# A four-layer attention and expert kernel: expert stages issued in a written order, two blocks a step, with up weights loaded three steps ahead

## The chip, the cores and the metric

The kernel runs on one core of one Trainium2 chip. The metric is the device time of one execution in microseconds (us), the median of several runs. Times inside the kernel come from one profiled execution. PE is the matmul engine (TensorE), DVE is VectorE, ACT is ScalarE, POOL is GpSimd, and SP is the engine whose queue issues the plain DMAs here.

## The reference, cut to what matters

`x` has 4 batches of 512 tokens of width 128; the context `ctx_1024` has 4 batches of 154 rows. Four layers each add an attention and an expert network to `x`, always on a normalised `x`:

```python
x = x + _L0_xattn_ref(_layernorm(x), ctx, ...)      # similarity of width 154, four feature groups @ W_qv
x = x + _L0_ffn_ref(_layernorm(x), ...)             # top 2 of 8; (x@W0+b0) * silu(x@W1+b1) @ W2 + b2, 512 hidden
x = x + _L1_xattn_ref(ctx, ctx, _layernorm(x), mask, ...)   # 16 heads of 8
x = x + _L1_ffn_ref(_layernorm(x), ...)             # top 1 with a capacity; gelu(x@W1+b1) @ W2 + b2, 512 hidden
x = x + _L2_xattn_ref(_layernorm(x), ctx, ...)      # 16 heads of 64, gated by tanh
x = x + _L2_ffn_ref(_layernorm(x), ...)             # top 2; gelu(x@w1) @ w2, 256 hidden, no biases
x = x + _L3_xattn_ref(_layernorm(x), ctx, ctx, ...) # 16 heads of 64
x = x + _L3_ffn_ref(_layernorm(x), ...)             # top 2; relu(x@W1+b1) @ W2 + b2, 512 hidden
```

All arithmetic on data is float32.

## The kernel before, in words

`x` lies in SBUF for the whole run, one tile per batch, four token tiles of 128 in each. A layer has these stages.

**Attention.** In layers 1 to 3 `attend_all` runs 16 periods, one for a token tile. A period (`narrow_period`, L431, for layer 1; `wide_period`, L486, for 2 and 3) writes out by hand the order of PE, ACT and DVE: scores and exponentials of the new tile beside transposes, the product with the values and the projection of the old one. `tc.manual_schedule` (L1280) keeps that order on PE, ACT and DVE. SP and POOL are placed by the framework. Each period also takes up to two steps of the work beside it (`middle`, `after`): the rest of the layer before, or the routing of the first half.

**Routing** (`route`, L647) for a half, which is two batches or 1024 tokens: statistics (L224 to L233, a power on POOL), normalisation (L240), transposes, logits (L662), the best one or two experts (`top`, L622), ranks, and from them a slot for each token in a buffer in DRAM that is sorted by expert and cut in blocks of 128. One expert owns a block. A list `eb` (L741) gives the expert of each block. The half has 23 blocks, in layer 1 it has 15. Sixteen indirect DMAs of 128 rows (8 in layer 1) scatter the tokens into the buffer (L718, on POOL). They are put in a list, `rows_due`, and `row_transfers` starts them two at a time, each behind some copy.

**Experts** (`experts`, L821). A block goes through `up` (L850): the expert's number is read into registers of SP and PE, its up weights are loaded with its biases behind them in the same rows (L861; 516 KB in layer 0, 258 KB in layers 1 and 3, 128 KB in layer 2; three buffers), and PE multiplies (L872) into `sc`, a PSUM tile of two banks, double buffered. Then `down` (L877): activation into `hT` (in layer 0 ACT computes silu from bank 1 of `sc`, L887, and DVE multiplies it with bank 0, L888; in layer 3 two pieces are done on DVE, L894, and two on ACT, L896), the product with the down weights (L899), a copy on DVE (`ys`, L907) and a store (L908). Every float32 product of 128x128 is two matmul instructions in the trace.

**Combining.** Sixteen indirect DMAs (8 in layer 1) gather the results (L932, on POOL) and DVE adds them to `x` with the weights of the experts (L950).

The halves overlap: the experts of half 0 run beside the routing of half 1, the experts of half 1 beside the gathers of half 0, the statistics and the preparation of the next attention. The gathers of half 1 run beside the next attention. Outside `attend_all` the framework's scheduler orders all engines, by readiness in a timeline of its own, so it may put an instruction of one stage between those of another.

**Constants.** Small parameters arrive in some 20 small DMAs; the context is transposed on PE (L193 to L202), some parameters too (L209, L1067, L1076).

The framework follows data in SBUF by regions and adds the waits between engines.

Of the kernel before, what the change touches and what calls it, by code (L numbers as in the profile page):

```python
# [9 lines left out]
F32 = mybir.dt.float32  # L10
# [36 lines left out]
def tile_xattn_moe_stack(ctx: ExitStack, tc: tile.TileContext, a: dict, out: bass.AP):  # L47
# [94 lines left out]
    wide_ends = const.tile([P, 4, P], F32, name="wide_ends")  # L142
    nc.gpsimd.memset(wide_ends, 0.0)
# [31 lines left out]
    nth = const.tile([1, BLK[0], E], F32, name="nth")  # L175
# [4 lines left out]
    def row_bc(src, n, name):  # L180

        t = const.tile([P, n], F32, name=name)
        nc.sync.dma_start(t, src.partition_broadcast(P))
        return t


    ctxT = const.tile([P, B, S2], F32, name="ctxT")
    ct4 = const.tile([P, B, 4, ST], F32, name="ct4")
    ct2 = const.tile([P, B, 64], F32, name="ct2")
    nc.gpsimd.memset(ct2, 0.0)  # L190
    tp = ps_tr()
    for b in range(B):
        nc.tensor.transpose(tp[:, b * P : (b + 1) * P], cm[:, b, :], ident)  # L193
    nc.vector.tensor_copy(ctxT[:, :, 0:P], tp.rearrange("p (b k) -> p b k", b=B))
    tp = ps_tr()
    for b in range(B):
        nc.tensor.transpose(tp[:, b * ST : (b + 1) * ST], ctail[:, b, :], ident[:ST, :ST])
    tpv = tp[:, 0 : B * ST].rearrange("p (b k) -> p b k", b=B)
    nc.vector.tensor_copy(ctxT[:, :, P:S2], tpv)
# [3 lines left out]

    def columns(src, rows, name):

        t = p2.tile([rows, P], F32, tag="rows", name=f"{name}_r")
        nc.sync.dma_start(t, src)
        q = ps_tr()
        nc.tensor.transpose(q[:, 0:rows], t, ident[:rows, :rows])  # L209
        o = const.tile([P, rows], F32, name=name)  # L210
        nc.vector.tensor_copy(o, q[:, 0:rows])
        return o
# [54 lines left out]
    class Tile:  # L267
# [8 lines left out]
        def __init__(self, at, i):  # L276
            self.at, self.i = at, i
            self.per = P // at.dh
            self.nb = H // self.per
            self.pr = p2.tile([P, H, S2], F32, tag="probs", name="probs")  # L280
            self.nm = small.tile([P, H], F32, tag="nm", name="nm")
            self.rs = small.tile([P, H], F32, tag="rs", name="rs")
            self.sc, self.q, self.pT, self.av = {}, {}, {}, {}
# [28 lines left out]
        def short(self):  # L312
            if self.nb == 1:
                self.ends = p2.tile([P, 4, T4], F32, tag="short", name="short", bufs=1)
                nc.scalar.copy(self.ends.rearrange("p g (h k) -> p (g h) k", h=4), self.pr[:, :, P:S2])
            else:
                self.ends = wide_ends
                for r in range(2):
                    nc.scalar.copy(
                        wide_ends[:, :, 64 * r : 64 * r + 2 * ST].rearrange("p c (s k) -> p c s k", s=2),  # L320
                        self.pr[:, 8 * r : 8 * r + 8, P:S2].rearrange("p (c s) k -> p c s k", s=2),
                    )
# [5 lines left out]
        def replicate(self):  # L328
# [5 lines left out]
            self.rep = p2.tile([P, self.nb, P], F32, tag="rep", name="rep")  # L334
# [21 lines left out]
        def take_ends(self, engine):  # L356
            self.tails = p2.tile([self.rows, 4, P], F32, tag="tails", name="tails")
            copy(engine, self.tails.rearrange("p g q -> p (g q)"), self.q["ends"][0 : self.rows, :])
# [72 lines left out]
    def narrow_period(new, old, middle=nothing, queries=nothing, parts=nothing, after=nothing):  # L431
# [37 lines left out]
        middle()  # L469
        if old:  # L470
            old.by_v(2)
            old.by_v(3)
            old.scaled(0)
        if new:
# [11 lines left out]
    def wide_period(new, old, middle=nothing, queries=nothing, parts=nothing, after=nothing):  # L486
# [24 lines left out]
        if old:  # L511
            old.scaled(0)
            old.by_v(3)
        middle()
        if old:
            old.scaled(1)
# [17 lines left out]
    def attention64(b, gather_x, wq, wk, wv, wo, add):  # L534
# [51 lines left out]
        def queries(i):  # L586
            at.qT[i] = t = p3.tile([P, 8, P], F32, tag="t8", name="qT")
# [49 lines left out]
    def row_transfers(n=2 * NH, behind=None):  # L637

        for start in rows_due[:n]:
# [6 lines left out]

    def route(layer, half, wg, bg, b2):  # L647
# [4 lines left out]
        lg = rsm("lg", NH, E)  # L652
# [18 lines left out]
        ohs, ws = [oh1], []  # L671
# [5 lines left out]
        else:  # L677
# [4 lines left out]
            ohs.append(oh2)  # L682
            nc.vector.tensor_tensor(sel[:, 0:NH, :], oh1, oh2, ALU.add)
# [18 lines left out]
        nc.vector.tensor_reduce(first, t4, AX.X, ALU.add)  # L702
        yield
        base = rsm("base", NH, E)
        nc.vector.scalar_tensor_tensor(base, bc(first, 1, NH), float(P), rk[:, 0:NH, :], ALU.mult, ALU.add)
        slots = []
# [8 lines left out]
        scatters = []  # L715
# [18 lines left out]
        end = rt.tile([1, E], F32, tag="end", name="end")  # L734
        nc.vector.tensor_tensor(end, first[0:1], nb[0:1], ALU.add)
        t6 = rt.tile([1, BLK[0], E], F32, tag="t6", name="t6", bufs=1)
        nc.vector.tensor_tensor(t6[:, 0:nj, :], bc(end, 1, nj), nth[:, 0:nj, :], ALU.is_le)
        ef = rt.tile([1, BLK[0]], F32, tag="ef", name="ef")
        nc.vector.tensor_reduce(ef[:, 0:nj], t6[:, 0:nj, :], AX.X, ALU.add)
        eb = rt.tile([1, BLK[0]], I32, tag="eb", name="eb")  # L740
        nc.vector.tensor_scalar(eb[:, 0:nj], ef[:, 0:nj], float(E - 1), None, ALU.min)  # L741

        if layer == 1:
# [9 lines left out]
            if half:  # L753
                nc.vector.tensor_tensor(rg, rk[:, 0:NH, :], bc(seen[0], 1, NH), ALU.add)
                nc.vector.tensor_tensor(rg, rg, oh1, ALU.mult)
            else:
                seen.append(tot)
                nc.vector.tensor_tensor(rg, rk[:, 0:NH, :], oh1, ALU.mult)
# [4 lines left out]
            ws.append(wa)  # L763
        else:
            d = rsm("d", NH)
            nc.vector.tensor_tensor(d, m2, m1, ALU.subtract)
# [8 lines left out]
            ws += [wa, wb]  # L775
        yield
        if b2 is not None:

            comb = rsm("comb", NH, E)
            nc.vector.tensor_tensor(comb, ohs[0], bc(ws[0], 2, E), ALU.mult)  # L780
            if len(ws) > 1:
                t7 = rsm("t7", NH, E)
                nc.vector.tensor_tensor(t7, ohs[1], bc(ws[1], 2, E), ALU.mult)
# [10 lines left out]
            for k, cT in enumerate(cTs):  # L794
                y = ps_av()
                for i in range(NI):
                    nc.tensor.matmul(
                        y[:, i * D : (i + 1) * D], cT[:, i * P : (i + 1) * P], b2, start=True, stop=True
                    )
                xb = x[2 * half + k]  # L800
                nc.vector.tensor_tensor(xb, xb, y.rearrange("p (i d) -> p i d", i=NI), ALU.add)
        return eb, list(zip(ws, slots)), scatters
# [11 lines left out]
    def load_down(layer):  # L814

        t = w1.tile([P, E, 4, D], F32, tag="w2", name="w2")
        nf = NF[layer]
        nc.sync.dma_start(t[:, :, 0:nf, :], a[f"down{layer}"].rearrange("p (e c d) -> p e c d", e=E, c=nf))
        return t

    def experts(layer, half, routed, w2):  # L821

        ebs, _, scatters = routed
        nj, nf, nu = BLK[layer == 1], NF[layer], UPS[layer]
        pack = a[f"up{layer}"]
        width = pack.shape[2]
        bias = nu * nf * P
        loaded, toks = {}, {}
# [12 lines left out]
        def tokens(g):  # L841
# [4 lines left out]
            tokT = wff.tile([P, 4 * P], F32, tag="tokT", name="tokT", bufs=2)  # L846
            evac(tokT[:, 0 : m * P], q[:, 0 : m * P])
            toks[g] = tokT

        def up(j):  # L850

            xT = toks[j // 4][:, (j % 4) * P : (j % 4 + 1) * P]
            e = nc.values_load(
                ebs[0:1, j : j + 1],
                engines=[mybir.EngineType.SP, mybir.EngineType.PE],
                min_val=0,
                max_val=E - 1,
                skip_runtime_bounds_check_because="a count of at most E - 1, by a minimum",
            )
            w = wff.tile([P, 1032], F32, tag="w", name="w")  # L860
            nc.sync.dma_start(w[:, 0:width], pack[bass.ds(e, 1), :, :].rearrange("o p n -> p (o n)"))  # L861
            sc = ps_sc()
            for u in reversed(range(nu)):
                for fc in range(nf):
                    at = (u * nf + fc) * P
                    if layer == 0:
                        dst = sc[:, u, fc * P : (fc + 1) * P]
                    elif layer == 3:
                        dst = sc[:, fc // 2, fc % 2 * P : (fc % 2 + 1) * P]
                    else:  # L870
                        dst = sc[:, 0, fc * P : (fc + 1) * P]
                    nc.tensor.matmul(dst, w[:, at : at + P], xT, start=True, stop=True)  # L872
            return e, w, sc
# [3 lines left out]
        def down(j, e, w, sc):  # L877
            hT = p3.tile([P, nf, P], F32, tag="hT", name="hT")
            if layer == 2:
                nc.scalar.activation(hT.rearrange("p f t -> p (f t)"), sc[:, 0, 0 : nf * P], AF.Gelu)  # L880
            for fc in range(nf if layer != 2 else 0):
                up = sc[:, 0, fc * P : (fc + 1) * P]
                b0 = w[:, bias + fc : bias + fc + 1]
                if layer == 0:
                    g = p2.tile([P, P], F32, tag="eg", name="eg", bufs=4)
                    b1 = w[:, bias + nf + fc : bias + nf + fc + 1]
                    nc.scalar.activation(g, sc[:, 1, fc * P : (fc + 1) * P], AF.Silu, bias=b1)  # L887
                    nc.vector.scalar_tensor_tensor(hT[:, fc, :], up, b0, g, ALU.add, ALU.mult)  # L888
                elif layer == 1:
                    nc.scalar.activation(hT[:, fc, :], up, AF.Gelu, bias=b0)  # L890
                else:
                    up = sc[:, fc // 2, fc % 2 * P : (fc % 2 + 1) * P]
                    if fc < 2:
                        nc.vector.tensor_scalar(hT[:, fc, :], up, b0, 0.0, ALU.add, ALU.max)  # L894
                    else:
# [491 lines left out]
```

## Time and profile before

| | |
|---|---|
| median of 3 runs | 1358.62 us (1355.46 to 1359.36) |
| the profiled execution | 1354.62 us |
| its span, first to last instruction | 1352.8 us |
| mean clock granted to PE | 0.93 |
| busy: PE, its weight loads, DVE, ACT, POOL | 1113.4, 908.6, 770.9, 568.8, 252.9 us |
| DMA | 126.81 MB, mean 94 GB/s |

The stages lie at these times in the trace, read from the first and last of their instructions:

| layer | attention | experts: first token transpose, half 0 | half 1 | first exponential of the next attention |
|---|---|---|---|---|
| 0 | 0 | 116.5 | about 204 | 291.7 |
| 1 | 291.7 | 512.1 | 562.0 | 605.0 |
| 2 | 605.0 | 846.1 | 908.4 | 955.3 |
| 3 | 955.3 | 1203.4 | 1267.6 | end 1352.8 |

In the profile "busy" is the time of instructions on an engine, "idle before" the time the engine stood still just before a group of instructions, and the name after the arrow is what that idle time ended with. Ends of matmuls are modelled, so a busy PE is not a PE at its peak.

### The profile page before, as it was taken

Reading aid. Unit: us, or ns where it says so; the run is one execution under the profiler, and the core shown is the slowest. Engines: PE = TensorE matmul, PEld = TensorE weight load, DVE = VectorE, ACT = ScalarE, POOL = GpSimd, SP = SyncE. Lnnn points to the kernel's source line nnn. Section 1 sums busy time; section 2 is a strip of 40 time slices with the busy share of each in tenths; the row PEclk is TensorE's granted clock in tenths of the full one; section 3 lists DMA queues with packets and bytes.
Section 4 is the critical chain, followed back from the end, with each engine's and each line's share of the span. In section 5 each row is a group of like instructions: output and inputs, shape, how many; then the busy total and the mean of one; then the engine's idle time right before and its main releaser. Section 6 shows DMA issues by size and latency. Waiting matters only on the chain.

```text
span 1352.8 us, 26947 instructions
## 1 busy us (share of the span) xinstructions
PE 1113.4 (82%) x9435; PEld 908.6 (67%) x9435; DVE 770.9 (57%) x2089; ACT 568.8 (42%) x2258; POOL 252.9 (19%) x281
## 2 busy tenths in 40 slices
PE   4885988887777788889999988868899998889891
PEld 3775887764334347777778777756777777679881
DVE  5563645557766764245666776425477576646452
ACT  1112443455454444455555455212555555433230
POOL 2022213104000020312000003045120000402424
PEclk8786998999898988998999999879999999989996
DMA  7013675551101214532112213444421111335762
GB/s 216 0 63 107 184 232 153 167 170 40 21 19 28 63 40 112 147 108 79 33 33 55 57 36 105 114 147 129 126 60 43 33 33 33 86 82 146 203 186 61
DMA packets 136995, 126.81 MB, mean 94 GB/s; under 512 B 13466, under 2 KB 116511, under 8 KB 136479
## 3 DMA queue, kind: packets, MB, share of 16 engines
q1 hardware_dynamic: 129695, 110.39, 29.4%
q0 software_dynamic: 7168, 14.69, 3.6%
q8 instruction: 78, 1.28, 0.4%
q14 instruction: 54, 0.44, 0.1%
HBM read 101.31 MB, written 23.72 MB: 92 GB/s over the span
## 4 chain that ended last, share of the span: by engine, by line
PE 35%; DVE 8%; DMA 6%; ACT 4%; issue 4%; POOL 3%; SPq 0%; POOLq 0%; DVEq 0%; ACTq 0%
PE sc L605 5%; PE tr L421 5%; PE av L404 4%; PE tr L367 4%; PE sc L872 4%; DMA w<-in_up 3%; PE av L899 3%; PE sc L590 3%; ACT probs L304 2%; DVE nm L292 2%; PE av L386 2%; DVE pT L261 2%; POOL yg L932 1%; PE sc L554 1%; POOL buf L718 1%
## 5 line engine op out<-in xcount | busy, mean ns | idle before, releaser
L304 ACT ACTIVATE probs<-sc,nm 128x154 f32<-128x154 f32 x768 | 286.1, 404 | 266.1 <-DVE nm L292 265.8
L872 PE MATMUL sc<-tokT,w 128*128 128x128 f32 x1528 | 213.9, 289 | 29.2 <-DMA w<-in_up 22.8
L872 PEld LDWEIGHTS sc<-tokT,w 128*128 128x128 f32 x1528 | 192.9, 200 | 43.3 <-issue 11.4
L899 PE MATMUL av<-w,hT 128*128 x1160 | 175.0, 284 | 11.4 <-DVE hT L888 8.5
L292 DVE TENSOR_REDUCE nm<-sc 128x6 f32<-128x924 f32 x144 | 142.9, 1009 | 68.1 <-PE sc L605 34.0
L304 ACT ACTIVATION_READ_ACCUMULATOR probs<-sc,nm 128x1 f32 x768 | 170.2, 222 | 0.0
L899 PEld LDWEIGHTS av<-w,hT 128*128 128x128 f32 x1160 | 150.4, 194 | 23.0 <-DVE hT L888 12.7
L932 POOL DMA_INDIRECT yg<-ybuf,su x112 | 107.6, 960 | 277.6 <-DVE pT L261 132.6
L261 DVE COPY pT<-tr 128x512 f32<-128x512 f32 x192 | 128.0, 687 | 52.3 <-PE tr L367 49.3
L233 POOL TENSOR_TENSOR rstd<-ve,nhalf 128x4 f32<-128x4 f32 x32 | 32.9, 1030 | 652.7 <-DVE ve L231 598.6
L718 POOL DMA_INDIRECT buf<-xn,su x112 | 108.1, 965 | 163.5 <-DVE eb L741 42.1
L367 PE MATMUL tr<-ident,probs 128*128 128x128 f32 x768 | 117.2, 287 | 13.3 <-DVE pT L261 13.3
L367 PEld LDWEIGHTS tr<-ident,probs 128*128 128x128 f32 x768 | 84.9, 144 | 40.3 <-DVE pT L261 20.4
L404 PE MATMUL av<-pT,vm 128*64 128x128 f32 (+1 forms) x1536 | 104.8, 286 | 7.1 <-DVE pT L261 7.1
L887 ACT ACTIVATE eg<-sc,w 128x128 f32<-128x128 f32 x184 | 66.2, 367 | 94.5 <-DVE hT L888 72.7
L907 DVE COPY ys<-av 128x128 f32<-128x128 f32 x168 | 48.5, 289 | 82.8 <-PE av L899 75.5
L888 DVE SCALAR_TENSOR_TENSOR hT<-sc,w,eg 128x128 f32<-128x128 f32 x184 | 63.0, 348 | 51.2 <-ACT eg L887 48.6
L404 PEld LDWEIGHTS av<-pT,vm 128*64 128x64 f32 (+1 forms) x1536 | 65.0, 128 | 35.9 <-issue 20.5
L605 PE MATMUL sc<-kT,qT 64*128 64x154 f32 x1024 | 85.1, 304 | 3.5 <-ACT probs L304 3.5
L605 PEld LDWEIGHTS sc<-kT,qT 64*128 64x128 f32 x1024 | 69.8, 186 | 13.3 <-ACT probs L304 7.7
L421 PE MATMUL tr<-wo,aT 128*128 128x128 f32 x512 | 67.1, 284 | 9.3 <-ACT tails L264 6.8
L590 PE MATMUL sc<-xnT,wq 128*128 128x128 f32 x512 | 71.0, 296 | 2.9 <-ACT probs L304 2.9
(251 smaller groups left out, 1460.6 us busy)
## 6 DMA issues: line engine op xcount, KB each, us to landing
w<-in_up SPq DMA_DIRECT2D x46, 516.0 KB
w<-in_up SPq DMA_DIRECT2D x76, 258.0 KB
rep<-rd SPq DMA_DIRECT2D x64, 256.0 KB
ybuf<-ys SPq DMA_DIRECT2D x168, 64.0 KB
tok<-buf SPq DMA_DIRECT2D x36, 256.0 KB
w<-in_down SPq DMA_DIRECT2D x3, 2048.0 KB
w<-in_up SPq DMA_DIRECT2D x46, 128.0 KB
buf<-zero SPq DMA_DIRECT2D x2, 1472.0 KB
```

The costliest lines, as they stand in the source:

```text
L261: return nc.vector.tensor_copy(o, i)
L292: nc.vector.tensor_reduce(self.at.heads(self.nm, g, n), self.sc[g][:, :, 0 : n * S2].rearrange("p j (s k) -> p j s k", s=n), AX.X, ALU.max ...
L304: nc.scalar.activation(self.pr[:, h, :], self.sc[g][:, j, s * S2 : (s + 1) * S2], AF.Exp, bias=self.nm[:, h : h + 1], accum_out=self.rs[:, ...
L367: nc.tensor.transpose(q[:, t * P : (t + 1) * P], self.pr[:, h, 0:P], ident)
L404: nc.tensor.matmul(av[rows, cols], v, self.pT[n][:, t, :], start=False, stop=last)
L421: nc.tensor.matmul(o[:, 0:D], self.aT[:, c, :], self.at.wo[:, c, :], start=(c == 0), stop=(c == self.nb - 1))
L590: nc.tensor.matmul(sc[:, c // 4, c % 4 * P : (c % 4 + 1) * P], wq[:, c * P : (c + 1) * P], at.xnT[:, i * P : (i + 1) * P], start=True, sto ...
L605: nc.tensor.matmul(sc[:, j, s * S2 : (s + 1) * S2], at.qT[i][rows, c, :], at.kT[rows, c, :], start=True, stop=True)
L718: ins = nc.gpsimd.indirect_dma_start(out=buf[half], out_offset=bass.IndirectOffsetOnAxis(ap=su[:, t : t + 1], axis=0), in_=xns[t // NI][:, ...
L872: nc.tensor.matmul(dst, w[:, at : at + P], xT, start=True, stop=True)
L899: nc.tensor.matmul(y[:, 0:D], hT[:, fc, :], w2[:, bass.ds(e, 1), fc, :].rearrange("p o d -> p (o d)"), start=(fc == 0), stop=(fc == nf - 1),)
L932: ins = nc.gpsimd.indirect_dma_start(out=yg[:, t, :], out_offset=None, in_=ybuf[half], in_offset=bass.IndirectOffsetOnAxis(ap=su[:, t : t ...
```

## The change

1. `tc.manual_schedule` now spans everything from the experts of layer 0 to the end. PE, ACT and DVE take the order in which the program writes the instructions; SP and POOL are still placed by the framework.
2. `experts` goes by steps: one block a step in layer 0, two in the others. `load_up` issues the weights three steps ahead into four buffers. Two blocks share one `sc` tile (a bank each), one PSUM tile of results, one copy and one store.
3. `activate` stands in the written order after the `down` of the step before, and so behind its copy. The copy is on ACT in layer 0, on DVE elsewhere. In layer 3 the first block's activation is all on DVE, the second's all on ACT.
4. Biases no longer come with the weights. All lie in SBUF, and `route` picks each block's by a multiplication and a sum on DVE for each hidden piece (8 in layer 0, 4 in layers 1 and 3).
5. The weights of the tokens and the bias of the second product move from `route` to `weigh`. For half 1 of layers 0 to 2 it runs beside the next attention.
6. Routing and preparation are cut into generator steps that run after each expert step, `pace` of them: 1, 3, 2, 2 in layers 0 to 3. Gathers go 2 (layer 0) or 4 behind each copy.
7. Constants are packed by the host into six arrays; the context, the output weights and the small query, key and value weights of layer 1 come transposed.
8. In the periods `middle` comes after `scaled`; buffers of `rep`, `tails`, `qT` and the probabilities are cut; the down weights are loaded in the second period.

```diff
+        def load_up(n):
...
+            ws[n] = w = wff.tile([P, per, width], F32, tag="w", name="w", bufs=4)
+            for i, j in enumerate(steps[n]):
+                es[j] = nc.values_load(
...
+                nc.sync.dma_start(w[:, i, :], a[f"up{layer}"][bass.ds(es[j], 1), :, :].rearrange("o p n -> p (o n)"))
...
+        def activate(blocks, sc):
+            hTs = [p3.tile([P, nf, P], F32, tag="hT", name="hT", bufs=4) for _ in blocks]
...
+                    if layer == 0:
+                        g = p2.tile([P, P], F32, tag="eg", name="eg", bufs=4)
+                        nc.scalar.activation(g, sc[:, 1, cols], AF.Silu, bias=bcol[:, j, nf + fc : nf + fc + 1])
+                        nc.vector.scalar_tensor_tensor(hT[:, fc, :], sc[:, 0, cols], b0, g, ALU.add, ALU.mult)
+                    elif layer == 1:
+                        nc.scalar.activation(hT[:, fc, :], sc[:, n, cols], AF.Gelu, bias=b0)
+                    elif n == 0:
+                        nc.vector.tensor_scalar(hT[:, fc, :], sc[:, n, cols], b0, 0.0, ALU.add, ALU.max)
+                    else:
+                        nc.scalar.activation(hT[:, fc, :], sc[:, n, cols], AF.Relu, bias=b0)
...
+            row_transfers(
+                2 * per, copy("s" if layer == 0 else "v", ys[:, 0:m, :].rearrange("p n d -> p (n d)"), y[:, 0 : m * D])
...
         load(0)
+        for n in range(3):
+            load_up(n)
         load(1)
         tokens(0)
         last = None
-        for j in range(nj):
-            this = (j, *up(j))
+        for n, blocks in enumerate(steps):
+            j = blocks[0]
+            load_up(n + 3)
+            sc = up(blocks, ws.pop(n))
             if last:
                 down(*last)
-            last = this
+            last = blocks, activate(blocks, sc)
```

```diff
+            for c in range(nc_):
+                t8 = rt.tile([P, BLK[0], E], F32, tag="t8", name="t8", bufs=1)
+                nc.vector.tensor_tensor(t8[:, 0:nj, :], begun[:, 0:nj, :], bc(biases[layer][:, c, :], 1, nj), ALU.mult)
+                nc.vector.tensor_reduce(r.biases[:, 0:nj, c], t8[:, 0:nj, :], AX.X, ALU.add)
...
+            pace = (1, 3, 2, 2)[layer]
+            first = Steps(experts(layer, 0, routed, weights)).step()
+            if last:
+                (narrow_period if layer == 1 else wide_period)(None, last)
+            if layer < 3:
+                prepare = setups[layer + 1]()
+            second = Steps(routing(layer, 1, layer == 3))
+            while not first.done:
+                first.step()
+                second.step(pace)
+            behind = second.finish()
+            row_transfers()
+            got = gather(0, routed, first.result)
+            second = Steps(experts(layer, 1, behind, weights))
+            while rows_due:
+                second.step()
+            second.step()
+            onto = Steps(onward(layer, 0, routed, got, prepare, found))
+            while not second.done:
+                second.step()
+                onto.step(pace)
```

## The prediction

> **What bounds the kernel now.** I read first the busy times of each stage, then who waits for whom, then the instructions in order of time in a quiet stretch of layer 0, then the groups on POOL. By stage (the columns are the stretch, its length, busy us of PE, of its weight loads, of DVE, ACT and POOL, the granted clock, the DMA share and GB/s):
>
> ```profile
> 114.00:205.00 91.00, 81.72 (x672) 78.05 (x673) 48.13 (x164) 41.23 (x105) 15.39 (x16) 0.95 0.62 189
> 205.00:290.00 85.00, 73.07 (x544) 66.25 (x542) 46.46 (x153) 32.57 (x91) 17.64 (x18) 0.96 0.56 166
> 512.00:605.00 93.00, 82.48 (x671) 75.72 (x673) 34.11 (x120) 42.01 (x135) 18.42 (x19) 0.95 0.47 132
> 846.00:956.00 110.00, 84.70 (x583) 74.11 (x581) 41.33 (x148) 27.17 (x62) 33.80 (x35) 0.86 0.45 130
> 1203.00:1325.00 122.00, 112.27 (x923) 104.11 (x922) 63.20 (x218) 33.12 (x101) 31.80 (x33) 0.99 0.61 166
> ```
>
> These are the expert stages of layers 0 (two halves), 1, 2 and 3. PE is idle in them for 9 + 12 + 11 + 25 + 10 = 67 us. No reordering of PE can win more than that, except at the ends. Layer 3 is near PE's limit; layer 2 is not. Who waits (us in total, times, longest):
>
> ```profile
> ACT eg L887 <- DVE hT L888: 72.7, 130, 4.0
> DVE hT L888 <- ACT eg L887: 48.6, 96, 4.3
> PE sc L872 <- DMA w<-in_up: 22.8, 31, 2.2
> ```
>
> Weights cost PE 23 us in all. The first two lines matter more. In layer 0 ACT reads bank 1 of `sc` and DVE bank 0, and each waits for the other:
>
> ```profile
> 272.23 0.37 ACT L887 ACTIVATE eg<-sc,w 128x128 f32<-128x128 f32 x1 [0.42 <-DVE hT L888]
> 272.63 0.35 DVE L888 SCALAR_TENSOR_TENSOR hT<-sc,w,eg 128x128 f32<-128x128 f32 x1 [0.43 <-ACT eg L887]
> 273.02 0.37 ACT L887 ACTIVATE eg<-sc,w 128x128 f32<-128x128 f32 x1 [0.42 <-DVE hT L888]
> 273.42 0.35 DVE L888 SCALAR_TENSOR_TENSOR hT<-sc,w,eg 128x128 f32<-128x128 f32 x1 [0.43 <-ACT eg L887]
> 273.81 1.06 PE L899 MATMUL av<-w,hT 128*128 x8
> 274.06 0.37 ACT L887 ACTIVATE eg<-sc,w 128x128 f32<-128x128 f32 x1 [0.67 <-PE sc L872]
> ```
>
> DVE must wait, since it uses ACT's result; but ACT also waits for DVE's last product before its next silu, though that reads another bank. Four pairs go in lock step, one each 0.785 us. The same shows where ACT and DVE copy out the halves of a query tile (DVE waits for ACT 24 times of 32). The first ACT line of the next block waits only for PE. So two engines take turns on one PSUM tile, by waits of the program, and the edit keeps that tile.
>
> [...] ACT's 128x512 copies took 0.585 us here[...].
>
> **Part 1, layer 0's turns.** Written order on ACT is now: copy `ys` of step n-1, then the four silus of step n. Behind the waiting copy stand all silus, and DVE's products wait for those, and PE's `down` for these. So there is one closed chain a block: last `hT` of n-1 to PE's weight load 0.05 (263.75 to 263.80 in the trace), the last pair of matmuls 0.50 to its modelled end, 0.04 to the copy (as DVE's copy has it)[...], four pairs 4 x 0.785 less a gap = 3.10. Sum **3.98, say 4.0 us a block**. PE's own issue is 24 x 0.112 = 2.7 us and hides behind it. Before, the scheduler put the copy on DVE among the pairs: blocks came each 2.7 to 3.5 us in quiet stretches, 3.54 us in the mean of half 0 and 3.90 of half 1.
>
> Pieces of routing on DVE fall into its gap of some 1.25 us between a block's last product and the next one's first. What is longer costs: statistics of two batches 2 x (4 x 0.28 + 4 x 0.17 + 0.17) = 3.9 us (+2.6), norms 2.3 (+1.0), bias picks 4 x (0.32 + 0.31) = 2.5 twice (+2.4; priced by the L737 and L739 rows of like size, 1x184), small ones 0.6: +6.6 us in half 0. In half 1 statistics and `kz` cost +2.5, and the preparation's own `sc` tile breaks the double buffer once, +1.5.
>
> Start: host-made constants take out eight transposes and two parameter turns. The first products now start at 14.8 us when `rhs` is ready; about 2 us come off, or nothing if packed DMAs queue (a row of 402 values to 128 partitions is 206 KB). I take the first block's copy at 123.4 for 126.8, since it no longer waits for the second block's loads. Then 123.4 + 22 x 4.0 + 6.6 = 218.0; next half's first copy after tokens, turn, up, activation and down +7.4 = 225.4; + 88 + 2.5 + 1.5 = 317.4; first exponential of layer 1 +2 = 319.4, against 291.7: **+27.7 us**. Table loads of 1.28 us that leave half 1's routing are inside this.
>
> **Part 2, layers 1 to 3.** Here PE leads a step: 32 matmuls x 0.112 = 3.6 us for two blocks in layers 1 and 3, plus transposes, 3.8 to 3.9; 1.8 in layer 2, where SP's registers and issues (2 x 0.70 + 0.33 + 0.19 = 1.9) bring it to 2.1. Layer 3's chain of copy 0.4, DVE 1.3, ACT 1.3, PE 0.55, gaps 0.15 is 3.7: it just fits. But the stages hang on another chain, on POOL:
>
> ```profile
> L932 POOL DMA_INDIRECT yg<-ybuf,su x112 | 107.6, 960 | 277.6 <-DVE pT L261 132.6
> L718 POOL DMA_INDIRECT buf<-xn,su x112 | 108.1, 965 | 163.5 <-DVE eb L741 42.1
> ```
>
> Sixteen of these take 16 x (0.96 + 0.30) = 20.2 us, and come in the order routing, scatter, half 1's tokens, gather, combine, next attention. The edit does not shorten them.
>
> *Layer 2* (before: scatter 884.0 to 904.1, tokens 908.4, gathers 914.9 to 934.7, exponential 955.3). The old period's tail now runs alone, residual at about 859.5. Statistics 3.9, power and norm to 867.5, evacuation and logits 871.2, two `top`s 874.4, ranks 877, slots 878.5; the first copy after that releases scatters at 879, to 899.4, tokens 904.6. First copy 909, gathers to 929.2, landed 931.4; combine and statistics 934.9, preparation behind three more steps to 945, exponential 948, +1.5 for shared `sc`: **-6**.
>
> *Layer 1*: with pace 3 the transposes of routing stand on PE behind the first two steps and wait for norms: PE idles 6 us, behind it all of `up` and `down`. Scatter about 551 to 560 (before 542.8 to 557), tokens 565 for 562, next exponential **+2**.
>
> *Layer 3*: the same way PE loses 3 + 3 + 1 us in routing, and the tail of 10.8 us isn't filled: half 0 ends near 1277 for 1269; half 1 at 3.8 a step gains back 6: **+2** at the last store, and the tail of 16 gathers stays as it was, 29 us.
>
> *Attention*: bias picks for half 0 (2.5 us in layers 1 and 3 each, 0.3 more for the list) and `weigh` come to the periods. DVE is busy 150 of 222 us there and PE 216 of 241, so much hides; free is the low end, 6 us the high; `middle` behind `scaled` takes up to 3 off. I take **+2**. Weights earlier: the 23 us of PE waiting are partly gone, but in layer 0 the turns and in layer 2 POOL come late instead. Register loads of PE (0.30 each) at a half's start: inside the numbers.
>
> **Sum**: 27.7 + 2 - 6 + 2 + 2 = +27.7. Profiled 1354.6 + 27.7 = 1382.3; the median of the runs is 4.0 above the profiled one, so **1386 us**. Own range 1366 to 1404: 4.0 may be 3.7 to 4.2 (44 blocks: -13 to +9), the other stages +-12.
>
> **Rivals.**
> - *No turns in layer 0* (chance 0.10). If the new order drops ACT's wait for DVE, the chain is 0.88 + 0.37 + 3 x 0.32 + 0.35 = 2.6 and PE's 2.7 leads: 44 x 1.3 = 57 less; some lost to DVE pieces (+12): 1386 - 45 = 1341, **faster**. It decides below about 3.4 us a block. For it: the data need no such wait. Against: the same two reads of one tile stand in the new text.
> - *Loads and pairs pay* (0.15). In layers 1 to 3 PE's waits for weights and tokens and POOL's late starts go without PE stalls in routing: two thirds of the 46 idle us there, and the losses of +4 gone: 1386 - 34 = 1352. For it: 25 idle us in layer 2. Against: POOL's 20.2 us twice.
> - *Periods slow down* (0.05): single `rep` and `tails` or larger pieces add 0.5 us to each of 48: 1410. The lifetimes don't overlap in the written order.
>
> **Chances.** A measurement can tell about 0.3%, 4 us, from no change. Main case 0.70. Faster: 0.10 + 0.08 of the second rival = 0.18; same 0.06; slower 0.76. The range 1349 to 1404 leaves out the first rival and the third, and some of the ends, under 0.2.
>
> **What would show it.** In layer 0: ACT copies `ys`, silus wait for it about 1 us a block, alternation stays, copies come each 4.0 us, first exponential near 319. Layer 2: scatters start near 879, next exponential 7 us earlier than before relative to the stage's start. If copies in layer 0 come each 3 us, or if scatters in layers 1 to 3 start 10 us earlier than before, I am wrong.

## The result and the profile after

The changed kernel takes 1421.01 us in the median of 4 runs (1414.94 to 1423.93), the one before 1357.04 us: a ratio of **1.047** (95% interval 1.042 to 1.053). The forecast was 1386, slower as measured, but 35 us short. The profiled execution took 1418.3 us. I cut both profiled executions into attention and expert stages: an expert stage runs from its layer's first token transpose to the next layer's first exponential (in layer 3 to the issue of the last store, 3 us before the span's end).

| us | att. 0 | exp. 0 | att. 1 | exp. 1 | att. 2 | exp. 2 | att. 3 | exp. 3 |
|---|---|---|---|---|---|---|---|---|
| before | 116.5 | 176.6 | 219.0 | 94.7 | 239.4 | 111.3 | 246.1 | 146.2 |
| after | 104.4 | 207.5 | 235.0 | 106.5 | 240.2 | 101.9 | 246.1 | 171.9 |
| difference | -12.1 | +30.9 | +16.0 | +11.8 | +0.8 | -9.4 | 0.0 | +25.7 |

The differences add up to 63.7 us, the whole of it. A second profile of the kernel after has 109.6 us for the first attention, so 5 us of its gain are not steady. Busy times by stage of the kernel after follow (stretch, length, PE, weight loads, DVE, ACT, POOL, granted clock, DMA share, GB/s); compare them with the first lines that the prediction shows of the kernel before:

```profile
104.00:205.00 101.00, 86.90 (x599) 76.51 (x599) 49.70 (x170) 37.69 (x113) 17.57 (x18) 0.93 0.45 145
205.00:312.00 107.00, 92.38 (x607) 76.71 (x609) 47.66 (x143) 42.98 (x127) 17.19 (x18) 0.93 0.49 160
547.00:653.00 106.00, 86.99 (x673) 78.73 (x673) 35.27 (x123) 38.67 (x130) 19.47 (x20) 0.88 0.42 127
893.00:995.00 102.00, 78.68 (x600) 70.09 (x599) 42.46 (x142) 22.47 (x58) 34.84 (x36) 0.88 0.53 157
1241.00:1389.00 148.00, 113.71 (x924) 107.39 (x923) 65.81 (x228) 28.94 (x97) 32.67 (x34) 0.95 0.47 139
```

In layer 3 PE has no more to do, 113.7 us where it was 112.3, but the stage is longer, so PE stands idle 34 us instead of 10. Who waits for whom (us in total, times, longest):

```profile
DVE hT L921 <- ACT eg L920: 101.2, 169, 4.3
...
ACT hT L927 <- DVE hT L925: 90.2, 17, 11.0
ACT eg L920 <- DVE hT L921: 65.8, 138, 2.1
...
PE sc L899 <- ACT tokT L92: 22.3, 14, 3.0
...
PE sc L899 <- DVE tokT L88: 17.1, 19, 2.1
```

PE's wait for `w` (22.8 us before) is gone from the list: the early weight loads do what they say. In its place stand 39 us of PE waiting for `tokT`, the token transposes that ACT or DVE copies out of PSUM (the evacuation), which the prediction had not priced. 24 of them lie in layer 3, 5 in layer 1. In the kernel before they were 2 us in all, and in layer 3's experts this one:

```profile
PE sc L872 <- DVE tokT L88: 0.3, 1, 0.3
```

The turns of ACT and DVE in layer 0 go on. POOL's groups are as they were:

```profile
L727 POOL DMA_INDIRECT buf<-xn,su x112 | 109.1, 975 | 340.6 <-DVE pT L261 170.6 <-DVE ys L261 31.8 <-DVE su L722 31.1
L980 POOL DMA_INDIRECT yg<-ybuf,su x112 | 106.7, 952 | 286.3 <-DVE pT L261 91.0 <-issue 57.4 <-ACT eg L920 46.7
```

**Layer 0.** ACT alone, in order of time, over one quiet block (no piece of routing beside it) of the kernel after (start, us, engine, line, operation; in brackets the idle time before it and what ended that):

```profile
278.34 0.27 ACT L264 COPY ys<-av 128x128 f32<-128x128 f32 x1 [0.96 <-PE av L936]
278.50 0.37 ACT L920 ACTIVATE eg<-sc,bcol 128x128 f32<-128x128 f32 x1
279.32 0.37 ACT L920 ACTIVATE eg<-sc,bcol 128x128 f32<-128x128 f32 x1 [0.44 <-DVE hT L921]
280.10 0.37 ACT L920 ACTIVATE eg<-sc,bcol 128x128 f32<-128x128 f32 x1 [0.42 <-DVE hT L921]
280.89 0.37 ACT L920 ACTIVATE eg<-sc,bcol 128x128 f32<-128x128 f32 x1 [0.42 <-DVE hT L921]
282.22 0.27 ACT L264 COPY ys<-av 128x128 f32<-128x128 f32 x1 [0.96 <-PE av L936]
```

From copy to copy 3.88 us, with the four turns and the wait for `down` of 0.96 us, as the closed chain of the prediction has it (4.0). The copy on ACT, the rest of its 3.98 us, stood in no trace then: DVE's took 0.289 us before (mean of 168), ACT's takes 0.27 here.

**Layer 3.** All engines over a long step of half 1, the same columns, some lines left out:

```profile
1333.75 0.60 PE L888 MATMUL tr<-ident,tok 128*128 128x128 f32 x4
...
1333.95 0.42 DVE L261 COPY ys<-av 128x256 f32<-128x256 f32 x1 [2.43 <-PE av L936]
1334.29 1.12 DVE L925 TENSOR_SCALAR hT<-sc,bcol 128x128 f32<-128x128 f32 x4
...
1335.51 1.14 ACT L927 ACTIVATE hT<-sc,bcol 128x128 f32<-128x128 f32 x4 [2.74 <-DVE hT L925]
...
1336.52 0.60 ACT L92 COPY tokT<-tr 128x512 f32<-128x512 f32 x1
...
1337.18 3.63 PE L899 MATMUL sc<-tokT,w 128*128 128x128 f32 x16 [2.82 <-ACT tokT L92]
```

PE transposes the next group's tokens at 1333.75 and could go on. But ACT's evacuation is queued behind four relus, these wait 2.7 us for DVE's four (both read one `sc` tile: the turns again), and DVE's stand behind the `ys` copy, which waits for `down`. PE stands 2.8 us. Then its matmuls take 0.22 us each where they took 0.11. The same stretch and the next by busy time (columns as above) show why:

```profile
1337.00:1340.50 3.50, 3.32 (x15) 3.33 (x16) 0.00 (x0) 0.12 (x1) 1.89 (x2) 0.51 0.47 142
1340.50:1342.30 1.80, 1.80 (x18) 1.80 (x17) 0.00 (x0) 0.00 (x0) 0.00 (x0) 1.00 0.28 46
```

The granted clock is 0.51 in the first stretch and 1.00 in the next; in the trace it is at half for 3.41 us from 1337.1, the end of the stall. So behind this stall of 2.8 us the `up` cost another 1.7 (3.63 us for 1.95). That the stall brings the fall isn't shown: of the stage's seven stalls of PE of 2.8 us or more two come with one, and behind the other five the clock stays at 1.00 (behind the one of 2.85 us that ends at 1359.01, 16 matmuls take 2.05 us). Steps of half 1 mostly alternate between 3.6 us and 6.0 to 7.1.

**Layer 1's experts.** The scatters of half 1 start 43.7 us after the stage's first transpose (590.6 from 546.9), before 30.7 (542.8 from 512.1). The stage's first step is followed in the written order by the whole last tile of the attention, and the second step waits behind it. Four events in order of time:

```profile
548.82 3.56 PE L899 MATMUL sc<-tokT,w 128*128 128x128 f32 x16 [0.83 <-DVE tokT L88]
...
558.79 2.02 PE L899 MATMUL sc<-tokT,w 128*128 128x128 f32 x16 [0.27 <-issue]
...
562.64 0.42 DVE L261 COPY ys<-av 128x256 f32<-128x256 f32 x1 [3.47 <-PE av L936]
...
565.94 2.49 PE L248 MATMUL tr<-ident,xn 128*128 128x128 f32 x8 [2.90 <-DVE xn L240]
```

From the start of the first `up` to that of the second 10 us pass; the norms of routing come only after the first copy.

### The profile page after: what moved, and what is told of

Its sections match the earlier page's. It is cut to its first block, busy times and chain, and to the rows that moved or that the text cites. A ratio compares the mean times of both kernels' runs of the same rounds, so it can differ in the third digit from the quotient of the medians.

```text
span 1416.6 us, 26418 instructions
## 1 busy us (share of the span) xinstructions
PE 1133.2 (80%) x9420; PEld 913.1 (64%) x9420; DVE 775.1 (55%) x2053; ACT 563.2 (40%) x2294; POOL 253.6 (18%) x281
## 4 chain that ended last, share of the span: by engine, by line
PE 56%; DVE 20%; ACT 12%; issue 7%; POOL 3%; DMA 2%; SPq 0%; POOLq 0%; ACTq 0%; DVEq 0%
PE sc L899 8%; PE av L936 7%; PE sc L606 5%; PE tr L369 5%; PE av L406 5%; PE tr L423 5%; DVE hT L921 4%; ACT eg L920 4%; PE sc L1178 4%; ACT probs L303 4%; DVE nm L291 3%; PE sc L591 2%; DVE pT L261 2%; PE av L388 2%; PE sc L1169 2%
## 5 line engine op out<-in xcount | busy, mean ns | idle before, releaser
L899 PE MATMUL sc<-tokT,w 128*128 128x128 f32 x1528 | 217.9, 301 | 45.1 <-ACT tokT L92 22.3
L899 PEld LDWEIGHTS sc<-tokT,w 128*128 128x128 f32 x1528 | 202.3, 213 | 59.4 <-ACT tokT L92 25.7
L936 PE MATMUL av<-w,hT 128*128 x1160 | 176.2, 290 | 22.8 <-DVE hT L921 19.4
L921 DVE SCALAR_TENSOR_TENSOR hT<-sc,bcol,eg 128x128 f32<-128x128 f32 x184 | 64.5, 350 | 101.3 <-ACT eg L920 101.2
L920 ACT ACTIVATE eg<-sc,bcol 128x128 f32<-128x128 f32 x184 | 67.9, 369 | 95.6 <-DVE hT L921 65.8
L261 DVE COPY ys<-av 128x256 f32<-128x256 f32 x64 | 26.3, 411 | 144.9 <-PE av L936 142.7
L423 PE MATMUL tr<-wo,aT 128*128 128x128 f32 x512 | 70.9, 296 | 8.2 <-ACT tails L264 6.1
L423 PEld LDWEIGHTS tr<-wo,aT 128*128 128x128 f32 x512 | 65.3, 207 | 14.2 <-ACT tails L264 8.2
```

Of the source, the lines that this page charges most:

```text
L261: return nc.vector.tensor_copy(o, i)
L423: nc.tensor.matmul(o[:, 0:D], self.aT[:, c, :], self.at.wo[:, c, :], start=(c == 0), stop=(c == self.nb - 1))
L899: nc.tensor.matmul(sc[:, u if nu > 1 else n, fc * P : (fc + 1) * P], w[:, n, (u * nf + fc) * P : (u * nf + fc + 1) * P], xT, start=True, s ...
L920: nc.scalar.activation(g, sc[:, 1, cols], AF.Silu, bias=bcol[:, j, nf + fc : nf + fc + 1])
L921: nc.vector.scalar_tensor_tensor(hT[:, fc, :], sc[:, 0, cols], b0, g, ALU.add, ALU.mult)
L936: nc.tensor.matmul(y[:, n * D : (n + 1) * D], hT[:, fc, :], w2[:, bass.ds(es[j], 1), fc, :].rearrange("p o d -> p (o d)"), start=(fc == 0) ...
```

## The experiments

Absolute times differ between chips (the first four ran where the kernel before took 1460.8 us, the others where it took 1350.2 to 1354.1), so times are compared as ratios to the kernel before on the same chip, stages within one group of runs. My theory after the result had four places: the turns in layer 0; `tokT` late in layer 3; routing late in layer 1; `weigh` in layer 1's attention. The rivals: the pairs of blocks and bias picks themselves, or the clock.

### Tokens one step earlier

```diff
-            if j % 4 == 2 and j // 4 + 1 in loaded:
+            if j % 4 == (2 if layer == 0 else 0) and j // 4 + 1 in loaded:
```

> Only change to the kernel after: in layers 1 to 3 the four token transposes and their evacuation for the next group of four blocks are written one step (two blocks) earlier. Theory T (the evacuation stands behind the whole activation of the step ahead, and the next step's up needs it): PE's waits for tokT, 39 us in the kernel after, fall below 10; layer 3's expert stage falls from 174.8 to about 148, layer 1's from 106.5 to about 98, layer 2's by 0 to 8; in all about -38 us, to some 1383. Rival P (two blocks a step are slow in themselves, or the weights are): layer 3 stays above 168, the sum within -8. Layer 0 (207.5 from first tokens to the first exponential) stays by both.

Measured: ratio 1.038 (1.034 to 1.042). Layer 3's expert stage 168.2 us, where the other three runs of the group have 182.6 to 186.2: some 16 to 18 less, between the two theories. Layer 1's stays (111.0 against 110.5 to 116.4). In layer 3 late tokens are a cause, in layer 1 hardly, and the 39 us of waits were no measure of the gain. On that chip engines show waits on something that the profile calls remote, up to 9.3 us (in the run with layer 0's copy on DVE), which runs on other chips lack, so the run was made again:

> The kernel after with the token transposes and evacuation of the next group one step (two blocks) earlier in layers 1 to 3, once more, since the first run of it was on a chip on which all kernels took 7% longer. Expected from that run: layer 3's stage 12 to 20 us less than the kernel after, layer 1's the same within 3 (it hangs on routing), in all 1.028 to 1.042 of the kernel before. If the theory's full size holds (all of PE's 39 us of waits for tokT come back), 1.02 or less.

Measured: 1.037 (1.028 to 1.045), layer 3's stage 155.9 for 171.9 (-16.0), layer 1's 104.1 for 106.5. Half 1 of layer 3 now has steps of 3.60 us in the mean, for 4.98; half 0, with routing in it, 5.72 for 6.04. PE's waits for `tokT` in layer 3 fall from 24.3 us to 1.6. Order of time in half 1:

```profile
1340.29 0.60 ACT L92 COPY tokT<-tr 128x512 f32<-128x512 f32 x1
...
1341.50 1.95 PE L899 MATMUL sc<-tokT,w 128*128 128x128 f32 x16
```

The evacuation ends at 1340.89, and that group's own `up` comes a step later; the `up` of 1341.50 needs nothing of it and has no wait in brackets. Its 16 matmuls take 1.95 us, at a granted clock of 1.00.

### Tokens in the same step, ahead of the activation

```diff
             sc = up(blocks, ws.pop(n))
+            if j % 4 == 2 and j // 4 + 1 in loaded:
+                tokens(j // 4 + 1)
+                load(j // 4 + 2)
             if last:
                 down(*last)
             last = blocks, activate(blocks, sc)
-            if j % 4 == 2 and j // 4 + 1 in loaded:
-                tokens(j // 4 + 1)
-                load(j // 4 + 2)
```

> The kernel after with the transposes of the next group in the same step as before, but ahead of that step's down, ys copy and activation instead of behind them (all layers). Theory T (the evacuation is late because it is queued behind the activation on ACT or DVE, not because it comes one step too late): it wins what the earlier step wins, layer 3's stage 12 to 20 us less, within 4 us of that run. Rival E (a whole step of lead is needed): less than half of it.

Measured: 1.037 (1.029 to 1.046), layer 3's stage 155.2 us. The same gain without a step of lead: the evacuation was late because it was queued **behind `down`, its copy and the activation** of the step. Rival E falls.

### Layer 0's gate half in a PSUM tile of its own

```diff
+            gate = ps_tr() if layer == 0 else None
...
+                        dst = gate if u else sc[:, 0 if nu > 1 else n]
...
-                        nc.scalar.activation(g, sc[:, 1, cols], AF.Silu, bias=bcol[:, j, nf + fc : nf + fc + 1])
+                        nc.scalar.activation(g, gate[:, cols], AF.Silu, bias=bcol[:, j, nf + fc : nf + fc + 1])
```

> Only change to the kernel after: in layer 0 the gate half of up goes to a PSUM tile of its own (one of the two tr tiles), so that ACT's silus and DVE's products read different tiles. Theory T (the turns on one sc tile set layer 0's step): ACT no longer waits for hT, copies come each 2.7 to 3.0 us in quiet blocks instead of 3.9, and layer 0's expert stage falls from 207.5 to about 165: about -40 us in all. Rival R (ACT's copy ahead of the silus or PE's order sets it): intervals stay above 3.6, the time within 8 us.

Measured: 1.028 (1.023 to 1.033); layer 0's experts 171.4 us, in the group's run with earlier tokens 207.7: -36. Quiet blocks come each 2.7 us, those with token transposes 4.3. The turns were what set the step of a quiet block.

### Layer 0's copy on DVE

```diff
-                2 * per, copy("s" if layer == 0 else "v", ys[:, 0:m, :].rearrange("p n d -> p (n d)"), y[:, 0 : m * D])
+                2 * per, copy("v", ys[:, 0:m, :].rearrange("p n d -> p (n d)"), y[:, 0 : m * D])
```

> Only change to the kernel after: layer 0's ys copy is on DVE instead of ACT. Theory T (one chain: down, copy, four turns): silus of the next block no longer stand behind the copy, the first of them runs beside down and copy, so a block falls from 3.9 to about 3.7 us: -5 to -12 us. Rival R (the copy on ACT is the whole loss against the kernel before): intervals fall to 3.3 or less, -25 us or more.

Measured: 1.046 (1.040 to 1.052); quiet blocks 3.5 us, layer 0's experts 200.4 (-7). The copy on ACT is a part of the chain, not the whole loss.

### weigh back in the routing

```diff
         if not hasattr(routed, "weights"):
             yield from weigh(routed)
+        else:
+            yield
+            yield
...
-            second = Steps(routing(layer, 1, layer == 3))
+            second = Steps(routing(layer, 1))
```

> Only change to the kernel after: the weights and b2 terms of half 1 are again formed inside the half's routing (beside half 0's blocks) in all layers, and two empty steps stand in their place in the next attention. Theory T (weigh in the first two periods of layer 1's attention puts PE's comb transposes and DVE's products ahead of the next tile's scores and PE's clock falls): the first five periods of layer 1, 79.1 us in the kernel after and 63.6 before, fall to 66 to 72; layer 0 grows by 2 to 4; in all -5 to -10 us. Rival G (late gathers, or the clock by itself): the five periods stay above 76, the time within 3 us.

Measured: 1.054 (1.050 to 1.058), no gain. The five periods fall from 90 to 91 in the group's other runs to 83.4 and the attention from 252 to 254 to 245.2, as theory T has it; but layer 0's experts grow by 10 (218.0, where 2 to 4 was expected) and layer 1's by 5 (116.4). The move gave with one hand and took with the other.

### The kernel after once more

> The kernel after, unchanged, as the yardstick of this group of runs, since absolute times differ between chips: 1.042 to 1.053 times the kernel before, with layer 3's expert stage the longest loss after layer 0's.

Measured: 1.050 (1.042 to 1.058), every stage but the first attention (109.6) within 0.4 us of the first profile.

### The scheduler back in the expert stages

The block under `with tc.manual_schedule(engines=ordered)` is taken out of it, and only this stays inside:

```diff
+            with tc.manual_schedule(engines=ordered):
+                routed, last, weights = attend_all(layer, prepare, found, at, beside)
```

> The kernel after with one thing undone: the written order holds in the attention periods alone, as in the kernel before, and the scheduler orders the expert stages; two blocks a step, loads three steps ahead, packed constants and bias picks stay. Theory T (the written order is the loss: the copy and the turns in layer 0, evacuation behind activation and routing behind steps in layers 1 and 3): layer 0's experts fall by 20 to 35 us, layer 1's by 8, layer 3's by 12 to 20, in all 1.00 to 1.015 times the kernel before. Rival P (pairs of blocks, bias picks or the loads lose it, whatever the order): over 1.035.

Measured: **0.976** (0.968 to 0.983), faster than both. Experts 163.7, 87.5, 95.8 and 139.4 us in layers 0 to 3: 44, 19, 6 and 32 less than after, in layers 0, 1 and 3 more than I expected, and all below before. In layer 1 half 1's scatters start 30.7 us after the first transpose, as before. The attention of layer 1 keeps its loss (232.8). So what the change brings beside the written order gains as a whole (pairs, early loads, bias picks and packed constants; how much each of them, no run tells), and the written order loses more than they gain.

### One block a step

`per` is 1 in all layers, layer 3's relus alternate by block, and `pace` is 1, 2, 1, 1.

> The kernel after with one block a step in layers 1 to 3 (written order stays; the token transposes of a group then stand a whole step ahead of their use; pieces beside a step are halved: 2, 1, 1). Theory T (tokens stand one step too late because a step is two blocks): layer 3's expert stage 12 to 20 us less than in the kernel after, PE's wait for tokT under 15 us, layer 1's about 0 to 4 less, layer 2's within 4; in all 10 to 22 us less. Rival W (the order itself is slow, with one block as with two): layer 3's stage within 5 us of the kernel after.

Measured: 1.026 (1.017 to 1.035). The median is 36 us below the kernel after on the same chip, where I expected 10 to 22. Layer 3's experts take 151.0 us (-21), layer 1's 95.8 (-10), layer 2's 101.8: layers 3 and 1 gain more than expected. In layer 1 the scatters start 10 us earlier in the stage. The attention's last tile now stands behind one block, not two, and the pace of 2 also gives four pieces of routing for two blocks instead of three; which of the two it is, this run doesn't tell.

### Six pieces of routing a step in layer 1

```diff
-                second.step(pace)
+                second.step(6 if layer == 1 else pace)
```

> The kernel after with six pieces of routing a step instead of three in layer 1's first half. Theory T (layer 1's stage hangs on routing, scatter, half 1's tokens, and routing comes late because its pieces stand behind the steps): scatters start 8 to 12 us earlier and the stage is 5 to 10 us shorter. Rival S (the steps themselves, PE at half clock and the waits for tokT, set it): scatters earlier, the stage within 3 us.

Measured: 1.044 (1.036 to 1.053). The scatters come 4.1 us earlier in the stage (8 to 12 expected), and the stage is 5.2 us shorter (100.9 for 106.1): its time follows the scatters, though more pieces a step bring less than I expected.

### Scheduled stages, and weigh in the routing

> The kernel with scheduled expert stages (0.976 of before), and half 1's weights and b2 terms formed inside its routing again, two empty steps in their place. Theory T (layer 1's attention lost 16 us to weigh on the chain of its first two periods, and to PE's clock after it): the first five periods fall from 76.7 to 63 to 70 and the attention from 232.8 to 219 to 226; layer 0's experts grow by 0 to 5; in all 4 to 12 us less. Rival C (the clock or other edits of the period: single buffers, middle behind scaled): the five periods stay above 73, and the time is the same within 4.

Measured: 0.981 (0.977 to 0.986). The five periods 68.2 us for 76.7 and the attention 224.7 for 232.8, as theory T has it; but layer 0's experts take 6 us more, layer 1's 7, and there is no gain in time. What `weigh` does in the period is read from the chain of waits of the kernel after (start, us, what):

```profile
318.37 0.11 ACT ex L796
318.47 0.02 issue
318.50 0.18 DVE u L798
318.68 0.02 issue
318.70 0.21 DVE wa L800
318.92 0.02 issue
318.94 0.17 DVE wb L802
319.11 0.18 DVE rinv L328
...
320.71 0.24 DVE comb L813
320.95 0.04 issue
320.99 1.87 PE tr L818 x8
322.86 0.77 PE sc L1169 x2
```

The exponential of `weigh` is queued behind the tile's, DVE's `rinv` behind its products, and the next tile's scores on PE behind its transposes (8 in 1.87 us; the granted clock is 0.50 from 316.6 to 326.8). In the run with `weigh` in the routing the same chain is short:

```profile
283.03 0.27 DVE rinv L328
283.30 0.04 issue
283.34 0.38 PE tr L333
283.73 0.77 PE sc L1169 x2
```

From `rinv` to the scores 0.7 us, with `weigh` 3.75.

### The same, and middle ahead again

> As the run with weigh in the routing and scheduled expert stages, and besides narrow_period calls middle ahead of by_v(2), by_v(3) and scaled(0) again, as in the kernel before. Theory T: middle's place is worth nothing in layer 1: its attention within 3 us of that run. Rival M (the move of middle holds the rest of layer 1's loss): its attention 4 to 10 us less than that run.

Measured: 0.976 (0.972 to 0.981). The attention is 219.4 us, 5.3 less and as long as before; the edit thus holds the rest of layer 1's loss in these two profiles. The first five periods stay (68.8 us), so it acts in the later ones. In time the two runs differ less than their intervals (layer 0's experts took 6.7 us longer here, though the edit doesn't touch them), so its worth is open.

### Scheduled stages with the own gate tile

> The kernel with scheduled expert stages, and layer 0's gate half in a PSUM tile of its own. Theory T (the turns still cost in a scheduled layer 0, but the scheduler fills them): layer 0's expert stage, 163.7 us scheduled and 171.4 with its own tile in written order, falls to 145 to 158. Rival N (PE leads a scheduled layer 0, 44 blocks at 2.7 and tokens): it stays at 160 to 166.

Measured: **0.960** (0.956 to 0.964), 1296.4 us, with layer 0's experts at 141.8, a little below the range. ACT and DVE in order of time:

```profile
161.04 1.14 ACT L923 ACTIVATE eg<-tr,bcol 128x128 f32<-128x128 f32 x4 [0.44 <-PE tr L901]
161.45 1.13 DVE L924 SCALAR_TENSOR_TENSOR hT<-sc,bcol,eg 128x128 f32<-128x128 f32 x4 [1.50 <-ACT eg L923]
```

Four silus take 1.14 us and four products 1.13, side by side, where each of four turns cost 0.785. ACT read one half of `sc` and DVE the other before too; what is new is that they are two tiles, so the turns came from the waits that the program keeps by tile.

### All three

> Scheduled expert stages, weigh in the routing, and the gate half in its own tile together. If the parts add up: 0.955 to 0.975 of the kernel before. If weigh's instructions fill what the turns left free, no better than the best of the two alone.

Measured: 0.960 (0.956 to 0.965), no better than the own tile alone: the second of the two cases.

### Written order with one block a step and the own gate tile

> Written order kept everywhere, with one block a step in layers 1 to 3 (1.026 of before by itself) and layer 0's gate half in a tile of its own (1.028 by itself). Theory T (two independent places of the written order lose it): the gains add up, layer 0's experts 171 and layer 3's stage 151: 0.99 to 1.01 of the kernel before, and still 15 to 40 us behind the scheduled stages. Rival O (any written order loses here): above 1.02.

Measured: 0.995 (0.992 to 0.997), 1343.4 us: by the ratios 70 to 75 us below after. The two parts add up (one block 36 us by itself; layer 0's experts 167.3, 40 less). A written order need not lose: the steps of two blocks and the shared tile held most of the loss. But the scheduled kernel with the same gate tile is ahead of it by 0.035 in the ratio, 47 us.

## Why the prediction was wrong

Term by term (its sum was +27.7, the profiles have +63.7):

- **Layer 0, right for the most part.** From first copy to the next exponential it had +31.1 (27.7 plus 3.4), the profiles show +31.8. Quiet blocks took 3.9 us where it had 4.0, half 0 95.8 where it had 94.6, the turn to half 1 9.9 for 7.4. The gate tile shows that the turns set it, the copy on DVE that the copy is in the chain. Its start was too late: for the first copy -3.4 was forecast, the profile has -13.0 (-7.8 in the repetition), so layer 0 ended at +18.8 rather than +27.7.
- **PE's idle time as a bound.** "No reordering of PE can win more than that" took busy PE time as work that must stay. In layer 0 PE was idle 21 us of the two halves, yet with scheduled stages and the own gate tile that stage is 35 us shorter, and PE is then busy 139.3 of 141.9 us where it was 157.8 of 176.6, with almost as many matmuls (1207 for 1229). A matmul's record is 0.275 us long there though matmuls start 0.11 us apart, so busy time covers short waits too.
- **Layer 2, right in sign:** -6 forecast, -9.4. Scatters start 3.5 us earlier in the stage, 5 forecast; where the rest comes from isn't followed here.
- **Layer 3, +2 forecast, +25.7: the step that failed most.** The prediction said "plus transposes, 3.8 to 3.9" a step and checked that the activation chain of 3.7 "just fits". It asked on which engine the activation runs, but not what is queued behind it. `tokens` is written behind `activate`, and with two blocks a step the next `up` needs its result. Steps of half 1 took 4.98 us; with the evacuation ahead, by either edit, 3.60 and 3.68, below the forecast. That is 16 of the 26 us. Against the kernel before, the run with early tokens still loses 9 us ahead of its first copy, 5 in the steps of half 0 and 6 between the halves, and gains 9 in half 1. The scheduled order is shorter by another 12 us in half 0's steps and 4 ahead of the first copy, while between the halves it loses as much; no run here divides this further.
- **Layer 1, +2 forecast, +11.8.** The mechanism was right (PE idles behind norms, the stage hangs on the scatters), the size wrong: tokens of half 1 were to come 3 us later, at 565 for 562, but the scatters came 13 us later in the stage. The last attention tile, with 10 us from the first `up` to the second, was left out there, while it was named for layer 3; no run takes it away by itself.
- **Attention, +2 forecast, +16.8, all in layer 1.** "So much hides" was argued from busy shares. `weigh` doesn't lie in the idle time; it stands ahead of `rinv` and of the next scores in an engine's queue. It costs some 8 us there, shown by the same edit in two orders, and saves 13 to 15 in the experts of layers 0 and 1, of which the forecast counted only the table loads. `middle` may hold another 5.
- **The clock** was in no term. The granted clock was at half for 61 us of layer 1's attention, before 38, for 30 of layer 0's experts, before 13, and in layer 3's experts, up to PE's last matmul, for 14, before 1. Part of the losses above may be this; how large a part isn't separated. In layer 3 it doesn't explain what the early tokens won: that run was 16 us shorter there, and its granted clock was 0.87 over half 0's steps, where the kernel after had 0.95, and 1.00 for 0.97 over half 1's.
- **The rivals.** "Loads and pairs pay" fits what comes with the order alone undone: the kernel is 0.976 of before, and the experts of layers 1 to 3 lie 30 us below before, though no run separates loads from pairs. In the kernel after the written order took it back. "No turns" was false in the kernel after, and is what the gate tile brings. "Periods slow down" put 0.5 us on each of 48 periods; the loss lay in layer 1's alone, and with `weigh` and `middle` undone nothing is left for the buffers (219.4 us for 219.0). Its "larger pieces" come nearest to what `weigh` does.

## What to carry to other kernels

When a written order replaces a scheduler, go through each engine's queue line by line and ask of every instruction what stands ahead of it and who waits behind it; a bookkeeping copy behind an activation is enough to stop the matmul engine (2.8 us here). Busy shares don't tell whether moved work hides: find the wait it would lie in. Give two engines that read different halves of one PSUM tile a tile each: here four turns of 0.785 us became 1.14 us beside 1.13.

## What the runs showed of the hardware

A second loss can come behind a PE stall: 2.8 us of waiting in layer 3 were followed by 3.5 us at a granted clock of 0.51, in which 16 matmuls took 3.6 us for 1.95. What brings such a fall isn't shown: five other stalls of 2.8 to 3.0 us in that stage were followed by a clock of 1.00, and in the kernel after 21 of the 32 falls to half clock had no stall of 2.8 us in the 7 us ahead, by the profile's ends of matmuls. ACT and DVE read two PSUM tiles side by side (1.14 and 1.13 us, starts 0.41 us apart) once each half was a tile, where in one tile a turn took 0.785 us. Waits in a list are no forecast of a gain: of PE's 39 us of waits for `tokT` 33 went when the evacuation came a step earlier, 23 of them in layer 3, but layer 3's stage became 16 us shorter and the whole profile 22.
